# A decoder layer on one Trainium2 core: h and x1 transposed by VectorE in 32x32 squares instead of by TensorE

## The chip, the cores and the metric

The kernel runs on one core of one Trainium2 chip. The metric is the device time of one execution in microseconds (us), and the time of the kernel before is the median of three runs. The engines that matter are TensorE (PE; its weight loads are shown apart as PEld), VectorE (DVE), ScalarE (ACT), GpSimd (POOL) and SyncE (SP). SP, ACT and POOL each have a queue from which they issue DMA transfers ("SPq", "ACTq", "POOLq"); an engine takes its instructions, and its DMA issues with them, in the order in which they are written.

## The reference

One decoder layer for 16 sequences of 112 rows (1792 rows in all, 1024 wide), in three steps, each closed by a layer norm:

```
s  = silu(x @ Wg.T);  of each row the 1376 smallest |s| of 2752 stay, the others become 0
h  = s * (x @ Wu.T)                        # 1792 x 2752
x1 = norm(x + h @ Wd.T)                    # 1792 x 1024
x2 = norm(x1 + attention(x1 @ Wq, keys and values of a context of 375) @ Wo)
out = norm(x2 + x2 @ W4.T)                 # W4: 4-bit weights, unpacked, in bfloat16
```

All but the last product is in float32.

## The kernel before

The rows are 14 tiles of 128. Every engine runs its instructions in the order in which the code writes them (`as_written`, line 83). The stages that the change touches:

**Up stage** (`up_chunk` and `turn` in `gates_keys_up`, from line 100). For each tile and each of six chunks of 512, 512, 352, 512, 512 and 352 columns, TensorE computes x @ Wu (line 234) from xT, the tile's transposed rows, which SP loads (line 138, two buffers) when the next chunk is the first of a tile. SP also loads the gate's chunk `us` and the mask `um` (lines 211 and 212), POOL multiplies them (line 213), and VectorE multiplies the product in (line 241). `turn(n)` then makes h transposed, because the next product needs its columns on the partitions: four or three TensorE transposes of 128x128 into PSUM (line 255), ScalarE copies (lines 257 and 261) and stores on POOL's queue into the DRAM tile `hT_d` (lines 258 and 262). `emit` (line 395) fixes the order: the turn of chunk n-3 first, then the loads for chunk n+1 and the matmuls of chunk n, then the evacuation (the VectorE product) of chunk n-1. The gate's chunk has four buffers, so the load of `us` for chunk n+1 waits until chunk n-3 has been turned.

All this runs beside the search for each row's threshold (`count`, `update`, `finish`, lines 278 to 356): 31 counting steps a tile on ScalarE (line 284) and VectorE (lines 287 to 296), two tiles in turn, and then some ten pieces of longer work on VectorE and POOL. `beside` (line 424) spreads the stream of matmul chunks over the steps, by the width of each; an up chunk counts 1.07 of its width.

**Down** (class `Down`, from line 471). h @ Wd goes over pairs of tiles with seven products in place of eight. `block` (line 526) loads half a tile of transposed h by two DMAs on SP. `last_pass` (line 652) does, pair by pair: `load_rest` (line 646; SP loads two blocks for the pair after this one, VectorE adds them, lines 553 and 554), a first product of 22 matmuls, two additions on VectorE (lines 683 and 684), the first layer norm (`norm`, line 670, which also stores x1 by POOL's queue), `load_rows` (two loads of x on SP), a second product, a subtraction (line 689), the second norm, row sums on POOL for the next pair (`add_rows`, line 668), and then the steps of `beside[j]`: the unpacking of the 4-bit weights on VectorE (`compute`, lines 716 to 730), loads on ACT's queue, and the first transposes of x1.

**Queries** (from line 735). `fetch` loads 112 rows of x1 (`xr`, ACT's queue, one buffer), `rows` transposes them by eight TensorE transposes (line 757) and two ScalarE copies (line 758) into `x1T`, and `chunk` multiplies by Wq (line 765). Two sequences make a group; the loop of `attention_and_ffn` (from line 1053) spreads fetches, transposes and chunks of the next group over its units. Ahead of it SP loads the first keys and values and Wo (lines 811, 815 and 999); scores are line 832, and the squares that VectorE already makes of the probabilities line 860, stored by DMAs of 32 partitions (line 874).

The lines that set the order in the up stage:

```python
        while len(to_turn) > 1:
            turn(to_turn.popleft())
        evacuate = what()
        if evacuate:
            behind.append((evacuate, at if at >= 0 else None))
            settle(1)
```

Of the kernel before, what the change touches and what calls it, by code (L numbers as in the profile page):

```python
# [10 lines left out]
F32 = mybir.dt.float32  # L11
# [6 lines left out]
ALU = mybir.AluOpType  # L18
AX = mybir.AxisListType
PSUM = bass.MemoryType.PSUM  # L20
DRAM = bass.MemoryType.DRAM

P = 128
B, S, D = 16, 112, 1024
NT = B * S
TT = NT // P
KC = D // P
# [3 lines left out]
Q = 32  # L31
NKQ = -(-SK // Q)
SKP = NKQ * Q
NKP = -(-SK // P)
NH, NKV, HD = 32, 8, 32
REP = NH // NKV
KVD = NKV * HD
GB = 2
GT = GB * S
# [60 lines left out]
def gates_keys_up(  # L100
    nc, tc, ident, xT, wg, wu, ctxT, wk, wv, s_d, m_d, hT_d, k_d, v_d, down, left, ps_g, ps_t
):
# [142 lines left out]
    def turn(n):  # L245

        t, c = ups[n]
        off, w = UP_CHUNKS[c]
        h = sm.pop((t, c))
        k0, nk = off // FH * HK + off % FH // P, -(-w // P)  # L250
        pt = ps_t.tile([P, 4, P], F32, tag="pt", name=f"pt_{t}_{c}")
        hT = io.tile([P, 4, P], F32, tag="hT", name=f"hT_{t}_{c}", bufs=2)
        for k in range(nk):
            r = min(P, w - k * P)
            nc.tensor.transpose(pt[:r, k, :], h[:, ds(k * P, r)], ident)  # L255
        whole = w // P
        nc.scalar.copy(hT[:, :whole, :], pt[:, :whole, :])
        nc.gpsimd.dma_start(hT_d[t][:, k0 : k0 + whole, :], hT[:, :whole, :])
        if nk > whole:
            r = w % P  # L260
            nc.scalar.copy(hT[:r, whole, :], pt[:r, whole, :])
            nc.gpsimd.dma_start(hT_d[t][:r, k0 + whole, :], hT[:r, whole, :])

# [112 lines left out]
    for n, (t, c) in enumerate(ups):  # L376
        stream.append((UP_CHUNKS[c][1] * 1.07, lambda n=n: up_chunk(n)))
    found, pieces = set(), deque()
# [92 lines left out]
class Down:  # L471
# [14 lines left out]

    def __init__(self, nc, tc, negh, wd, hT_d, x, x1_d, ps):
        self.nc, self.tc, self.negh, self.wd, self.hT_d = nc, tc, negh, wd, hT_d
        self.x, self.x1_d, self.ps = x, x1_d, ps
        self.pairs = TT // 2  # L490
        self.parts = {"11": [], "21": []}
        self.asked = [(b, k) for b in ("11", "21") for k in range(HK)]
        self.n_blocks = 0
        self.live = {}
# [31 lines left out]
    def block(self, t, h):  # L526

        pool = (self.a1, self.a2)[self.n_blocks // 4 % 2] if self.a2 else self.a1
        self.n_blocks += 1
        a = pool.tile([P, HK, P], F32, tag="h", name=f"h_{self.n_blocks}", bufs=4)  # L530
        h_d = self.hT_d[t]
        self.nc.sync.dma_start(a[:, :FULL, :], h_d[:, ds(h * HK, FULL), :])
        self.nc.sync.dma_start(a[:REST, FULL, :], h_d[:REST, h * HK + FULL, :])
        return a
# [8 lines left out]
    def product(self, bank, a, b):  # L543
        for k in range(HK):
            r = P if k < FULL else REST
            self.nc.tensor.matmul(  # L546
                bank, a[:r, k, :], b(k)[:r],
                start=(k == 0), stop=(k == HK - 1),
            )
# [86 lines left out]
    def load_sums(self, j):  # L636

        v = self.nc.vector
        a11, a12, a21, a22 = (self.block(2 * j + i, h) for i in range(2) for h in range(2))
        self.combine(v, a22, a21, a22, ALU.add)  # L640
        self.combine(v, a21, a11, a21, ALU.subtract)
        self.combine(v, a22, a22, a11, ALU.subtract)
        self.combine(v, a12, a12, a22, ALU.subtract)
        self.live[j] = a22, a21, a12

    def load_rest(self, j):

        a21, a22 = (self.block(2 * j + 1, h) for h in range(2))
        self.combine(self.nc.vector, a21, a21, a22, ALU.add)
        self.live[j] = a21, a22  # L650

    def last_pass(self, beside):

        nc = self.nc
        with ExitStack() as ctx:
# [14 lines left out]
            def norm(j, i, y):  # L670
                layer_norm(nc, small, y, y, self.negh)
                nc.gpsimd.dma_start(self.x1_d[ts(2 * j + i, P), :], y)

            rows = {0: load_rows(0)}
            add_rows(0, rows[0])
            for j in range(self.pairs):
# [7 lines left out]
                nc.vector.tensor_add(y1[:, 512:], y1[:, 512:], p)  # L684
                norm(j, 0, y0)
                if j + 1 < self.pairs:
                    rows[j + 1] = load_rows(j + 1)
# [47 lines left out]
class Queries:  # L735


    def __init__(self, nc, tc, ctx, ident, x1_d, wq_sb, bank):
        self.nc, self.ident, self.x1_d, self.wq_sb, self.bank = nc, ident, x1_d, wq_sb, bank
        self.pool = ctx.enter_context(tc.tile_pool(name="q_work", bufs=1, side="right"))  # L740
        self.x1T, self.qT, self.xr = {}, {}, {}

    def fetch(self, g, bb):

        self.xr[g, bb] = self.pool.tile([S, D], F32, tag="xr", name=f"xr_{g}_{bb}")
        self.nc.scalar.dma_start(self.xr[g, bb], self.x1_d[ds((g * GB + bb) * S, S), :])

    def rows(self, g, bb):
        nc = self.nc
        if bb == 0:  # L750
            self.x1T[g] = self.pool.tile([P, KC, GT], F32, tag="x1T", name=f"x1T_{g}")
            self.qT[g] = self.pool.tile([P, KC, GT], F32, tag="qT", name=f"qT_{g}", bufs=2)
        xr = self.xr.pop((g, bb))
        for k0 in range(0, KC, 4):
            pt = self.bank()[:, : 4 * S].rearrange("p (k s) -> p k s", k=4)
            for k in range(4):
                nc.tensor.transpose(pt[:, k, :], xr[:, ts(k0 + k, P)], self.ident[:S, :S])  # L757
            nc.scalar.copy(self.x1T[g][:, k0 : k0 + 4, ts(bb, S)], pt)  # L758

    def chunk(self, g, mc):  # L760

        nc = self.nc
        pq = self.bank()
        for kc in range(KC):
            nc.tensor.matmul(  # L765
                pq[:, :GT], self.wq_sb[:, kc, ts(mc, P)], self.x1T[g][:, kc, :],
                start=(kc == 0), stop=(kc == KC - 1),
            )
        nc.scalar.activation(self.qT[g][:, mc, :], pq[:, :GT], AF.Copy, scale=SCALE)


def attention_and_ffn(nc, tc, ident, ident_b, negh, x1_d, k_d, v_d, queries, wf_sb, wo, out):
# [16 lines left out]
    with ExitStack() as ctx:  # L789
# [213 lines left out]
        asked, behind, light = deque((0, mc) for mc in range(EARLY, KC)), deque(), {}  # L1003
        turned, fetched = GB, GB
        sums, tails = {}, {}
# [47 lines left out]
        for n in range(n_units):  # L1053
# [16 lines left out]

            if not asked and turned < B and n >= (turned // GB - 1) * per_group:
                queries.rows(turned // GB, turned % GB)
                turned += 1
                if turned % GB == 0:
                    asked.extend((turned // GB - 1, mc) for mc in range(KC))
            if fetched == turned < B:
                queries.fetch(fetched // GB, fetched % GB)
                fetched += 1
            lights(n)
# [41 lines left out]
def kernel(  # L1121
# [30 lines left out]
    v_d = dram.tile([B, SKP, KVD], F32, tag="v", name="v_d")  # L1152
    x1_d = dram.tile([NT, D], F32, tag="x1", name="x1_d")

    hT_d = [dram.tile([P, 2 * HK, P], F32, tag=f"h{t}", name=f"hT_d{t}") for t in range(TT)]
    with as_written(nc, tc):
        with ExitStack() as psum:
            ps_g = psum.enter_context(tc.tile_pool(name="ps_g", bufs=6, space=PSUM))
            ps_t = psum.enter_context(tc.tile_pool(name="ps_t", bufs=2, space=PSUM))
            with ExitStack() as left:  # L1160
                down = Down(nc, tc, negh, wd, hT_d, x, x1_d, ps_g)
                gates_keys_up(
                    nc, tc, ident, xT, wg, wu, ctxT, wk, wv, s_d, m_d, hT_d, k_d, v_d, down, left,
                    ps_g, ps_t,
                )
# [3 lines left out]
                wf_sb = a_w.tile([P, 8, D], BF16, tag="wf", name="wf_sb")  # L1169
                queries = Queries(nc, tc, ctx, ident, x1_d, wq_sb, lambda: down.bank("pq"))  # L1170
                with tc.tile_pool(name="q", bufs=2, side="right") as q_pool:
# [4 lines left out]
                    loads, computes = unpack_steps(nc, q_pool, wf_sb, qw, qs, qz)  # L1176
                    beside = [[] for _ in range(TT // 2)]
                    for i, j in enumerate((1, 1, 2, 3, 4, 4, 5, 6)):
                        beside[j].append(computes[i])
                    for i, j in enumerate((0, 0, 1, 1, 2, 3, 4, 4)):  # L1180
                        beside[j].append(loads[i])
                    for i in range(4):
                        beside[i // 2].append(lambda i=i: load_wq(i))
                    beside[4].append(lambda: queries.fetch(0, 0))
                    beside[5] += [lambda: queries.rows(0, 0), lambda: queries.fetch(0, 1)]
                    beside[6].append(lambda: queries.rows(0, 1))
                    down.last_pass(beside)
            for mc in range(EARLY):
# [50 lines left out]
```

## Time and profile before

| | |
|---|---|
| median of three runs | 2656.92 us (2655.61 to 2657.28) |
| the profiled execution | 2661.48 us |
| its span, first to last instruction | 2659.7 us |
| PE busy | 2584.9 us (97%) |
| DVE busy | 1730.8 us (65%) |
| ACT busy | 1377.6 us (52%) |
| POOL busy | 1053.8 us (40%) |
| mean granted TensorE clock | 0.983 |
| up stage, by TensorE's order of time | 853.1 to 1404.7 us |
| last pass | 1735.3 to 1891.0 us |
| first scores of attention | 1901.95 us |

The profile is of one execution. Its page gives the busy time of each engine, the span in 40 slices, the DMA queues, the chain of work that ended last, and the costliest groups of instructions; the trace behind it can be asked for the order of time on each engine ("timeline": start, duration, and in brackets the idle time in front and what ended it), for the waits, and for the busy time and clock in any window. A group's line names the kernel's line, the engine, the operation and the tiles. TensorE's ends are modelled; its pitch, from start to start, is the safer number. A float32 matmul is two instructions.

### The profile page before, as it was taken

The page shows a single profiled execution, that of the slowest core. Times are in us where ns is not written, and L with a number is a line of the kernel's source. Part 1 is how long each engine was busy: PE and PEld are TensorE (multiplying, and loading weights), DVE is VectorE, ACT ScalarE, POOL GpSimd, SP SyncE. Part 2 cuts the span into 40 slices and gives each one's busy share as a digit, 9 for nine tenths or more (in the row PEclk, how much of TensorE's full clock was granted, in tenths as well). Part 3 has the DMA queues.
Part 4 walks back from the last instruction along what each step waited for, and adds up shares of the span by engine and source line. Part 5 has one row for each costly group of instructions (what it writes and reads, how often), then busy time and mean ns, then how long its engine had stood idle before and what let it go on. Part 6 is the DMA issues. An engine that isn't in the chain of part 4 may idle for free.

```text
span 2659.7 us, 33179 instructions
## 1 busy us (share of the span) xinstructions
PE 2584.9 (97%) x10266; PEld 1482.7 (56%) x10266; DVE 1730.8 (65%) x3579; ACT 1377.6 (52%) x2413; POOL 1053.8 (40%) x1097
## 2 busy tenths in 40 slices
PE   9999999999999999999999999998899999999997
PEld 4444444577776555555554444443556666667663
DVE  0478778866876788788730343158467777777773
ACT  0487787777767777787610000000255555565553
POOL 0002022213322444344450000023277888788783
PEclk9999999999999999999999999999889999999998
DMA  6221223154443543443346222166567777777763
GB/s 253 94 74 56 77 91 126 51 195 168 181 169 136 162 140 121 143 132 117 95 145 228 86 96 94 59 204 202 133 169 196 196 191 193 192 205 194 188 175 103
DMA packets 216960, 387.70 MB, mean 146 GB/s; under 512 B 32080, under 2 KB 151120, under 8 KB 212688
## 3 DMA queue, kind: packets, MB, share of 16 engines
q1 hardware_dynamic: 165456, 257.19, 32.3%
q0 software_dynamic: 35840, 100.59, 11.6%
q10 hardware_dynamic: 15488, 27.80, 3.5%
q8 instruction: 83, 1.36, 0.2%
q14 instruction: 93, 0.76, 0.1%
HBM read 208.36 MB, written 76.43 MB: 107 GB/s over the span
## 4 chain that ended last, share of the span: by engine, by line
PE 90%; DVE 3%; DMA 3%; ACT 2%; issue 1%; POOL 1%; ACTq 0%; SPq 0%; POOLq 0%; DVEq 0%
PE pg L146 20%; PE pu L234 19%; PE m L546 14%; PE bank L924 7%; PE pk L184 6%; PE pk L176 6%; PE bank L765 6%; PE sc L832 4%; PE po L887 3%; PE bank L975 2%; PE pt L255 1%; ACT probs L840 1%; DVE b L727 1%; DMA xr<-x_d 1%; DVE nmax L838 1%
## 5 line engine op out<-in xcount | busy, mean ns | idle before, releaser
L284 ACT ACTIVATE ja<-a,cand 128x1824 int8<-128x1824 f32 x434 | 788.6, 1817 | 178.4 <-DVE cand L296 174.4
L287 DVE TENSOR_SCALAR_CACHE_REDUCE jv<-a,cand 128x928 uint8<-128x928 f32 x434 | 510.0, 1175 | 56.9 <-ACT a L271 48.8
L234 PE MATMUL pu<-wu_sb,uxT 128*128 128x512 f32 (+1 forms) x1344 | 530.6, 548 | 0.0
L146 PE MATMUL pg<-wg_sb,gxT 128*128 128x456 f32 (+1 forms) x1344 | 519.9, 550 | 5.9 <-DMA wg_sb<-in_wg_dram 5.9
L840 ACT ACTIVATE probs<-sc,nmax 128x375 f32<-128x375 f32 x512 | 287.4, 573 | 237.6 <-DVE nmax L838 218.2
L146 PEld LDWEIGHTS pg<-wg_sb,gxT 128*128 128x128 f32 x1344 | 256.2, 191 | 268.8 <-issue 265.3
L849 POOL TENSOR_TENSOR probs<-probs,sums 128x1500 f32<-128x1500 f32 x128 | 344.2, 2689 | 142.4 <-DVE sums L848 123.2
L234 PEld LDWEIGHTS pu<-wu_sb,uxT 128*128 128x128 f32 x1344 | 249.0, 190 | 230.0 <-issue 188.4
L838 DVE TENSOR_REDUCE nmax<-sc 128x2 f32<-128x750 f32 x256 | 228.6, 932 | 150.3 <-PE sc L832 150.2
L546 PE MATMUL m<-wd,h 128*128 128x512 f32 (+1 forms) x616 | 268.0, 597 | 0.0
L860 DVE STREAM_TRANSPOSE squares<-probs 128x1536 f32<-128x1536 f32 x128 | 224.0, 1750 | 9.7 <-DMA weights<-squares 5.5
L155 POOL DMA_DIRECT2D s_d<-s x84 | 46.0, 548 | 427.4 <-DVE s L154 351.5
L765 PE MATMUL bank<-x1T,wq_sb 128*128 128x224 f32 x976 | 202.6, 361 | 0.0
L546 PEld LDWEIGHTS m<-wd,h 128*128 128x128 f32 (+1 forms) x616 | 117.5, 191 | 149.2 <-issue 145.1
L765 PEld LDWEIGHTS bank<-x1T,wq_sb 128*128 128x128 f32 x976 | 181.3, 191 | 33.2 <-issue 30.2
L924 PE MATMUL bank<-wo_sb,aT 128*128 128x256 f32 x832 | 195.0, 388 | 0.0
L758 ACT COPY x1T<-pq 128x448 f32<-128x448 f32 x4 | 2.0, 535 | 371.6 <-PE pq L757 371.6
L874 POOL DMA_DIRECT2D weights<-squares x320 | 178.6, 564 | 9.0 <-issue 6.6
L924 PEld LDWEIGHTS bank<-wo_sb,aT 128*128 128x128 f32 x832 | 155.4, 192 | 46.5 <-issue 24.9
L184 PE MATMUL pk<-wv_sb,ctx 128*128 128x256 f32 (+1 forms) x768 | 168.4, 379 | 0.0
L176 PE MATMUL pk<-ctx,wk_sb 128*128 128x375 f32 x512 | 164.4, 478 | 0.0
L184 PEld LDWEIGHTS pk<-wv_sb,ctx 128*128 128x128 f32 (+1 forms) x768 | 144.0, 188 | 24.8
(118 smaller groups left out, 2881.8 us busy)
## 6 DMA issues: line engine op xcount, KB each, us to landing
weights<-squares SPq DMA_DIRECT2D x704, 96.0 KB, 3.3
h<-hT_d SPq DMA_DIRECT2D x56, 640.0 KB, 4.5
weights<-squares POOLq DMA_DIRECT2D x320, 96.0 KB, 3.4
ctx<-in_ctxT_dram SPq DMA_DIRECT2D x16, 1500.0 KB, 6.7
a<-s_d SPq DMA_DIRECT2D x14, 1376.0 KB, 7.9
us<-s_d SPq DMA_DIRECT2D x56, 256.0 KB, 2.7
hT_d<-hT POOLq DMA_DIRECT2D x56, 256.0 KB, 3.1
s_d<-s POOLq DMA_DIRECT2D x56, 228.0 KB, 2.2
```

Source lines behind the costliest of these rows:

```text
L146: nc.tensor.matmul(pg[:, :w], xts[t][:, kc, :], wg_sb[:, kc, ds(off, w)], start=(kc == 0), stop=(kc == KC - 1),)
L176: nc.tensor.matmul(pk[:, :SK], wk_sb[:, kc, ts(u, P)], c[:, kc, :], start=(kc == 0), stop=(kc == KC - 1),)
L184: nc.tensor.matmul(pk[:n, :KVD], c[:, kc, ds(at, n)], wv_sb[:, kc, :], start=(kc == 0), stop=(kc == KC - 1),)
L234: nc.tensor.matmul(pu[:, :w], xts[t][:, kc, :], wu_sb[0][:, kc, ds(off, w)], start=(kc == 0), stop=(kc == KC - 1),)
L284: nc.scalar.activation(ja, a[:, NV:], AF.Sign, bias=cand, scale=-1.0, accum_out=st["sgn"])
L287: nc.vector.tensor_scalar(jv, a[:, :NV], cand, -(TOPK - 1 - NA / 2), ALU.is_lt, ALU.add, accum_out=st["nlt"])
L546: self.nc.tensor.matmul(bank, a[:r, k, :], b(k)[:r], start=(k == 0), stop=(k == HK - 1),)
L765: nc.tensor.matmul(pq[:, :GT], self.wq_sb[:, kc, ts(mc, P)], self.x1T[g][:, kc, :], start=(kc == 0), stop=(kc == KC - 1),)
L838: nc.vector.tensor_reduce(nmax[h], sc[h][:, :, :SK], AX.X, ALU.max, negate=True)
L840: nc.scalar.activation(pr[:, i, :SK], sc[i // 2][:, i % 2, :SK], AF.Exp, bias=nmax[i // 2][:, i % 2 : i % 2 + 1], accum_out=sums[:, i : i ...
L849: nc.gpsimd.tensor_tensor(pr, pr, sums.unsqueeze(2).to_broadcast([P, 4, SK]), ALU.mult)
L924: nc.tensor.matmul(pp[:, :256], aT[:, h, r, :], wo_sb[:, h * REP + r, ts(i, 256)], start=(h == 0 and r == 0), stop=(h == 1 and r == REP - 1),)
```

## The change

- `turn` no longer uses TensorE. VectorE transposes each 32x32 square of the chunk (one instruction, two for the 352-wide chunks), writing with a step of 4 or 3 elements so that the squares of a row lie together; POOL sets the padding of the last chunk to zero; four DMAs of 32 partitions, two on SP's queue and two on POOL's, put the squares into place in `hT_d`. The two PSUM buffers of the transposes go to the matmuls (6 to 8), and an up chunk counts its plain width in the stream.
- A block of h is loaded by one DMA, its columns are read by the down products with a step of 4 or 3 elements, and sums over blocks are one instruction instead of two.
- `norm` in the last pass transposes x1 too: two VectorE instructions a tile, into dead accumulators, and eight DMAs on SP's queue into a new DRAM tile `x1T_d`. The transposes, copies and fetches of Queries go; `load` takes a whole group by one DMA on ACT's queue, and the loop asks for it when the chunks of the group before are all written.
- The unpacking stands between the two products of a pair (`amid`, after the first norm), no longer behind the second norm.

```diff
@@ turn
-        pt = ps_t.tile([P, 4, P], F32, tag="pt", name=f"pt_{t}_{c}")
-        hT = io.tile([P, 4, P], F32, tag="hT", name=f"hT_{t}_{c}", bufs=2)
-        for k in range(nk):
-            r = min(P, w - k * P)
-            nc.tensor.transpose(pt[:r, k, :], h[:, ds(k * P, r)], ident)
-        whole = w // P
-        nc.scalar.copy(hT[:, :whole, :], pt[:, :whole, :])
-        nc.gpsimd.dma_start(hT_d[t][:, k0 : k0 + whole, :], hT[:, :whole, :])
...
+        at, whole, nk = off % FH, w // P, -(-w // P)
+        tile = io.tile([P, 512], F32, tag="hT", name=f"hsq_{t}_{c}", bufs=2)
+        sq = tile[:, : nk * P].rearrange("p (m f k) -> p m k f", m=SQ, k=nk)
+        nc.vector.transpose(
+            sq[:, :, :whole],
+            h[:, : whole * P].rearrange("p (k m f) -> p m k f", m=SQ, f=Q),
+        )
         if nk > whole:
...
+            n = w % P // Q
+            nc.gpsimd.memset(sq[:, n:, whole], 0.0)
+            nc.vector.transpose(
+                sq[:, :n, whole], h[:, whole * P : w].rearrange("p (m f) -> p m f", f=Q)
+            )
+        n = nk * Q
+        to = hT_d[t].rearrange("(m p) h n -> p m h n", p=Q)
+        for b in range(SQ):
+            queue = (nc.sync, nc.gpsimd)[b % 2]
+            queue.dma_start(
+                to[:, :, off // FH, ds(at + b * n, n)],
+                tile[ts(b, Q), : nk * P].rearrange("p (m n) -> p m n", m=SQ),
+            )
@@ the stream
-        stream.append((UP_CHUNKS[c][1] * 1.07, lambda n=n: up_chunk(n)))
+        stream.append((UP_CHUNKS[c][1], lambda n=n: up_chunk(n)))
@@ Down.block, Down.product
-        self.nc.sync.dma_start(a[:, :FULL, :], h_d[:, ds(h * HK, FULL), :])
-        self.nc.sync.dma_start(a[:REST, FULL, :], h_d[:REST, h * HK + FULL, :])
+        self.nc.sync.dma_start(a, self.hT_d[t][:, h])
...
+            at, n = k // 4 * 4 * P, min(4, HK - k // 4 * 4)
             self.nc.tensor.matmul(
-                bank, a[:r, k, :], b(k)[:r],
+                bank, a[:r, ds(at + k - at // P, P, n)], b(k)[:r],
@@ Down.last_pass
             def norm(j, i, y):
                 layer_norm(nc, small, y, y, self.negh)
-                nc.gpsimd.dma_start(self.x1_d[ts(2 * j + i, P), :], y)
+                t = 2 * j + i
+                nc.gpsimd.dma_start(self.x1_d[ts(t, P), :], y)
+                to = self.x1T_d.rearrange("(m p) b k f -> p m b k f", p=Q)
+                n = KC // 2
+                for h in range(2):
+                    sq = ((self.c11[j], self.v[j]), (self.u[j], None))[i][h]
+                    if sq is None:
+                        sq = ld.tile([P, 512], F32, tag="sq", name=f"x1sq_{t}", bufs=1)
+                    sq = sq.rearrange("p (m k f) -> p m k f", m=SQ, f=Q)
+                    nc.vector.transpose(
+                        sq, y[:, ts(h, 512)].rearrange("p (k m f) -> p m k f", m=SQ, f=Q)
+                    )
+                    for b in range(SQ):
+                        nc.sync.dma_start(to[:, :, t * SQ + b, ts(h, n)], sq[ts(b, Q)])
...
                 norm(j, 0, y0)
+                for step in amid[j]:
+                    step()
                 if j + 1 < self.pairs:
                     rows[j + 1] = load_rows(j + 1)
@@ Queries (fetch and rows go)
+    def load(self, g):
+        n = GT // Q
+        self.x1T[g] = self.pool.tile([P, n, KC, Q], F32, tag="x1T", name=f"x1T_{g}")
+        self.nc.scalar.dma_start(self.x1T[g], self.x1T_d[:, ts(g, n)])
...
-                pq[:, :GT], self.wq_sb[:, kc, ts(mc, P)], self.x1T[g][:, kc, :],
+                pq[:, :GT].rearrange("p (b f) -> p b f", f=Q), self.wq_sb[:, kc, ts(mc, P)],
+                self.x1T[g][:, :, kc, :],
@@ the loop of attention_and_ffn
-            if not asked and turned < B and n >= (turned // GB - 1) * per_group:
-                queries.rows(turned // GB, turned % GB)
-                turned += 1
-                if turned % GB == 0:
-                    asked.extend((turned // GB - 1, mc) for mc in range(KC))
-            if fetched == turned < B:
-                queries.fetch(fetched // GB, fetched % GB)
-                fetched += 1
+            if not asked and group < B // GB:
+                if group not in queries.x1T:
+                    queries.load(group)
+                elif n >= (group - 1) * per_group:
+                    asked.extend((group, mc) for mc in range(KC))
+                    group += 1
@@ tile_decoder_kernel
-            ps_g = psum.enter_context(tc.tile_pool(name="ps_g", bufs=6, space=PSUM))
-            ps_t = psum.enter_context(tc.tile_pool(name="ps_t", bufs=2, space=PSUM))
+            ps_g = psum.enter_context(tc.tile_pool(name="ps_g", bufs=8, space=PSUM))
...
                     for i, j in enumerate((1, 1, 2, 3, 4, 4, 5, 6)):
-                        beside[j].append(computes[i])
+                        amid[j].append(computes[i])
...
-                    beside[4].append(lambda: queries.fetch(0, 0))
-                    beside[5] += [lambda: queries.rows(0, 0), lambda: queries.fetch(0, 1)]
-                    beside[6].append(lambda: queries.rows(0, 1))
+                    beside[4].append(lambda: queries.load(0))
```

## The prediction

> **What bounds the kernel now.** I read the chain of work that ended last first, then TensorE's order of time in each stage, then the queue that feeds it (SyncE), then VectorE. The page's chain:
>
> ```profile
> PE 90%; DVE 3%; DMA 3%; ACT 2%; issue 1%; POOL 1%; ACTq 0%; SPq 0%; POOLq 0%; DVEq 0%
> ```
>
> TensorE carries the end nearly everywhere, so an instruction taken from it is worth its pitch, and a new wait of TensorE costs its full length. Its order of time at one tile boundary of the up stage (start, duration; 3-4 transposes stand between the chunks):
>
> ```profile
> 1115.44 7.03 PE L234 MATMUL pu<-wu_sb,uxT 128*128 128x512 f32 x16
> ...
> 1122.64 4.90 PE L234 MATMUL pu<-wu_sb,uxT 128*128 128x352 f32 x16
> 1127.38 0.60 PE L255 MATMUL pt<-ident,us 128*128 128x128 f32 x4
> 1127.81 7.03 PE L234 MATMUL pu<-wu_sb,uxT 128*128 128x512 f32 x16
> ```
>
> SyncE and VectorE at the same place: the next tile's xT is issued when TensorE starts chunk 4 of the old tile (1115.4), 11.3 us before its use at 1127.81; VectorE does chunk 4's product only at 1130.39, 7.9 us after TensorE ended it (1122.5).
>
> ```profile
> 1116.48 0.42 SPq L138 DMA_DIRECT2D uxT<-in_xT_dram  x1
> ```
> ```profile
> 1130.39 0.66 DVE L241 TENSOR_TENSOR us<-us,pu 128x512 f32<-128x512 f32 x1
> ```
>
> VectorE lags because the search's last pieces (3.1, 1.6, 1.6, four of 1.6 us ...) come in a bunch. Today that lag costs nothing, since SyncE waits for TensorE's transposes, hardly for VectorE (its queue's waits between 870 and 1330: total, times, longest):
>
> ```profile
> SPq L211 <- PE pt L255: 358.0, 69, 6.4
> SPq L212 <- DMA m_d<-m: 12.5, 1, 12.5
> SPq L211 <- DVE us L241: 10.8, 9, 2.9
> ```
>
> The last pass, and its one long stall:
>
> ```profile
> 1735.33 114.19 PE L546 MATMUL m<-wd,h 128*128 128x512 f32 x264
> 1868.20 1.73 PE L757 MATMUL pq<-ident,xr 112*128 112x112 f32 x8 [18.68 <-DMA xr<-x_d]
> 1869.72 21.43 PE L546 MATMUL m<-wd,h 128*128 128x512 f32 x44
> ```
>
> Six pairs take 114.2 us dense (a pair of 44 matmuls 18.9, by the chain's 359.15 us for 836); then the x1 transposes that stand in front of the last pair wait 18.7 us, and the clock, at 0.50 to 0.55 from 1865 to 1875 by the windows, makes the last pair 2.5 us longer.
>
> **The change part by part.** Durations are of the profiled execution (2661.5 us; span 2659.7); it is 4.6 above the median of 2656.9, and I put the differences on the median.
>
> *Up stage, removed.* From 853.1 to 1404.7 is 551.6 us; the matmuls alone are 28 x (6.87+6.87+4.74) = 517.4. The transposes are the rest: -34 us. ScalarE's 112 copies (L257, L261) go too; ScalarE is no bound, worth nothing.
>
> *Up stage, added: VectorE's squares.* The only row of such an instruction:
>
> ```profile
> L860 DVE STREAM_TRANSPOSE squares<-probs x128: 1741/1748/1779, 1916.1 to 2607.0; 128x1536 f32<-128x1536 f32 x128
> ```
>
> 1.75 us for 1536 elements, about 0.14 of it fixed: 0.67 for 512, at a pitch of 0.60 (as L241, of the same size: 0.69, pitch 0.60), some 3.4 us a tile. Its squares leave in runs of 32; the new ones leave with a step of 3 or 4 elements, which no VectorE row shows. Ends: 0.60, and 1.22 by the slowest VectorE row per element (the scan L334, 1.64 for 688); faster than L860's rate is excluded, since nothing here is narrower. I take 0.60: L860 is the same operation. Beside POOL's work L860 never grows (1779 at most).
>
> *Up stage, moved: SyncE.* Two of four stores of each chunk now stand on SyncE, waiting for VectorE, and the load of the next tile's xT is queued behind those of chunk 2. The instruction order shows VectorE turning chunk 2 directly in front of its product of chunk 4. So xT can be issued only when VectorE gets to chunk 4's product, plus two issues of 0.60 (L874, the nearest DMA of 32 partitions; low end 0.32 of L211), plus 4.9 to land: reach + 6.1 us. I held that against the start of the next tile on TensorE in the trace of before. At five boundaries VectorE is early (idle 1 to 2 us in front of the product): no stall. At the others the product starts at 888.67, 970.35, 1050.46, 1130.39, 1164.74, 1202.36, 1242.56 and 1323.47, and the next tile at 891.71, 970.41, 1049.11, 1127.81, 1167.16, 1206.51, 1245.86 and 1324.56: with 6.1 added TensorE would wait 3.1, 6.0, 7.5, 8.7, 3.7, 2.0, 2.8 and 5.0, in all 39 us. In the three long lags VectorE also has about 0.6 more and TensorE 0.4 less a chunk, over four chunks: 3 x 4 = 12. Together about +50 (25 if xT lands in the fastest 3.8 and the issues are 0.32, so that each wait is 1.7 shorter and VectorE's squares find room; 75 with squares of 1.2 and the 2.5 us of slow clock behind each long stall). **Net of the stage: +16.** The lighter weight of an up chunk (1.07 to 1.0) gives 3% more search to the gate stage, where VectorE is 71 to 82% busy: nothing. The padding (28 memsets) and 56 more POOL issues at 0.55 us fall on a POOL 40 to 52% busy: nothing, unless the squares wait for them.
>
> *The strided weights.* The down products read h with a step of 12 or 16 bytes. Nearest rows: L968 loads strided weights (step 16 bytes, bf16) in 150 ns, L975 contiguous ones in 103. In that ratio 190 becomes 277 ns, under the 427 ns pitch of a 512 matmul: nothing; a gain is excluded, since the load is already hidden. Uncovered from 427 ns on. Queries' moving operand in runs of 32: L887 does so at 391 ns against 388 of L924: nothing. The Trainium skill, "SBUF — State Buffer", section "Door 1: The DMA port swizzle", says that SBUF is read in lines of 16 bytes and that each access to a new line pays; it speaks against both strides. It gives no price; by it the squares would sit at their dear end and the sum at 2708 below, by L860's row it stays at 2671.
>
> *Last pass.* PE loses the stall. But SyncE gets 16 stores a pair, and the loads of the pair after next (load_rest) stand behind the last eight, which wait for VectorE's squares of the pair's second norm; VectorE's next instruction is the sum of just these loads. That closes a loop, per pair: sum 1.6, adds and first norm 4.4 (1745.05 to 1749.45), squares 1.3, unpack 4.3 each (1895.04 to 1899.4, without POOL's rows beside it), second norm 3.9, first square 0.7, eight stores 4.8, load 0.4+4.5+0.4: 22 us + 4.3 per unpack, against TensorE's 18.9. Counted from the pass's start (1735.3): third pair's sum ready at 35, then 66 (two unpacks), 92, 118, 149 (two): last pair starts at 149, not 113. POOL's row sums for it (behind the norms of the pair before) end at about 167; from there 4.4 + 1.3 + 4.3 + 3.9 + 0.7 bring its last norm's squares to 182, eight stores to 187, and only then does SyncE load the first keys: first scores at 190. Before: 1901.95 - 1735.3 = 167. **+23** (issue 0.33: +11; if SyncE never blocks: first scores at 132 + 9.4 + 0.5 = 142, **-25**). Unpacking away from POOL's row sums (5.7 us for an L727 that takes 0.69 alone) is worth 5 us an unpack on VectorE and is in the loop.
>
> *Attention.* 14 groups of eight transposes, 0.87 apart from what follows, go (-12), and waits for xr of 10.7 us, with some 2 us of slow clock behind the longest (matmul groups of 1.76 and 1.63 for 0.93 and 0.91): **-25**. x1T is fetched as one load when the last chunk has read the old one, one to three units ahead; a unit is 4 to 6 us, a load of 896 KB some 6 to 9 (512 KB: 5.1): I take nothing, end +8.
>
> **Sum:** +16 +23 -25 = +14: 2657 + 14 = **2671 us**.
>
> **Rivals.**
> - *Neither queue wait shows* (SyncE's stores are quick, VectorE's lag shrinks with ScalarE's freed copies): -34 -25 -25 = -84: 2573. For it: VectorE is idle 16 to 20% of the up stage. Against: the lag at the boundaries stands in the trace. 0.08.
> - *One of the two shows*: xT alone (+16 -25 -25): 2623, or the last pass alone (-34 +23 -25): 2621. It ends faster, and decides it where one loop is short: xT landing within 3.8 and issued at 0.32 each leaves only three boundaries late. 0.20.
> - *VectorE becomes the bound*: at squares of 1.2 us the up stage has 84 x 0.6 = 50 us more VectorE work, of which some 20 fall in lags, and the last pass 28 x 0.6 = 17 in its loop: 2671 + 20 + 17 = 2708. It decides from squares of about 1 us. 0.14.
> - *The forecast*, both waits, 2634 to 2704 by its bounds (-34 +25 +11 -25 and -34 +75 +23 -17): 0.58.
>
> **How the numbers follow.** 0.2% (5.3 us) is about what a measurement of this kernel can tell from no change: 2651.6 to 2662.2. Of the forecast's 0.58, 0.41 lies above, 0.11 inside, 0.06 below. Slower 0.41+0.14 = 0.55; same 0.11; faster 0.06+0.20+0.08 = 0.34. Range 2615 to 2715: it leaves out the first rival and a little above.
>
> **What would show it.** TensorE idle in front of chunk 0 of tiles 2, 4 and 6 on uxT, 5 to 10 us each, with half clock after: if it is idle nowhere between 853 and 1390 the second step is wrong. TensorE idle 7 to 12 us in front of pairs 3 to 6 on VectorE's sum of h, and SyncE idle on the squares; kT as the first scores' releaser. L256 at 0.67 us for 512, or more. L757 gone and no wait on x1T in attention. Wrong I should be if a DMA is not held by those in front of it on SyncE, or the landing times differ by a few us.

## The result, and the profile after

The changed kernel takes 2775.62 us (median of 4 runs, 2774.39 to 2777.74), the kernel before 2657.1 us beside it (2655.61 to 2659.72): ratio 1.0446, 95% interval [1.0428, 1.0464]. The forecast of 2671 us had the sign right and the size far too small; the range ended at 2715. In the profiled executions the spans are 2772.6 and 2659.7 us, 112.9 apart, and the stages divide them so (from TensorE's order of time; the up stage is counted to the first down product):

| us | up stage | first passes | last pass to first scores | attention | span |
|---|---|---|---|---|---|
| before | 551.6 | 330.6 | 166.6 | 757.8 | 2659.7 |
| after | 622.2 | 330.8 | 208.5 | 758.0 | 2772.6 |
| difference | +70.6 | +0.2 | +41.9 | +0.2 | +112.9 |
| forecast | +16 | 0 | +23 | -25 | +14 |

The chain of work that ended last, on the page after:

```profile
PE 66%; DVE 11%; DMA 8%; issue 4%; POOL 4%; ACT 3%; SPq 3%; ACTq 0%; DVEq 0%; POOLq 0%
```

It was 90% TensorE; a third of the time (34%, a tenth before) now runs through other engines' work, much of it in front of a waiting TensorE. Before, TensorE had no wait in front of a matmul of the up stage; now it waits at nine tile starts, 84.5 us in all (total, times, longest):

```profile
PE pu L235 <- DMA uxT<-in_xT_dram: 59.9, 5, 19.2
PE pu L235 <- DVE hsq L256: 20.3, 3, 8.7
PE pu L235 <- DVE rej L306: 4.4, 1, 4.4
```

What SyncE's queue waited for between 870 and 1330 us (total, times, longest), where it used to wait for TensorE's transposes:

```profile
SPq L270 <- DVE hsq L263: 131.7, 21, 13.4
SPq L270 <- DVE hsq L256: 89.1, 23, 9.0
SPq L270 <- DVE us L242: 78.4, 16, 13.1
SPq L270 <- POOL hsq L262: 29.0, 6, 10.0
```

The first three are the forecast's step: stores waiting for VectorE. The fourth is not in it. L262 is the padding of the last chunk's squares, set to zero by POOL. One of the three longest waits of TensorE, from four orders of time around 1060 us (VectorE's squares of a chunk 2 from after's line 263; POOL; SyncE; TensorE):

```profile
1059.07 0.26 DVE L263 STREAM_TRANSPOSE hsq<-us 128x96 f32<-128x96 f32 x1
```
```profile
1065.25 1.48 POOL L358 TENSOR_TENSOR e<-e,c 128x688 bf16<-128x688 bf16 x1
1066.81 1.49 POOL L359 TENSOR_TENSOR m<-m,e 128x688 bf16<-128x688 bf16 x1
1068.59 0.60 POOL L361 DMA_DIRECT2D m_d<-m  x1 [0.30 <-POOL m L359]
1069.19 0.16 POOL L262 MEMSET hsq<- 128x32 f32 x1
```
```profile
1069.37 1.99 SPq L270 DMA_DIRECT2D hT_d<-hsq  x2
1071.45 0.39 SPq L139 DMA_DIRECT2D uxT<-in_xT_dram  x1
```
```profile
1076.35 6.17 PE L235 MATMUL pu<-wu_sb,uxT 128*128 128x512 f32 x8 [18.62 <-DMA uxT<-in_xT_dram]
```

The squares were done at 1059.3. Their store could not go before the padding was set, the padding stood on POOL behind the search's masks (eight of 1.49 us), and xT stood on SyncE behind the store: the store goes out 10.0 us late, and xT with it, for an instruction that takes 0.16. It happens again at 1378 and 1431, 7.3 and 16.1 us late, in front of waits of 19.25 and 13.18 us. Meanwhile TensorE's granted clock falls to 0.53 (1060 to 1076 us).

VectorE's squares of h and of x1 (the second row is one of the four groups of L694):

```profile
L256 DVE STREAM_TRANSPOSE hsq<-us x84: 503/1091/1161, 876.6 to 1480.3; 128x512 f32<-128x512 f32 x56, 128x256 f32<-128x256 f32 x28
```
```profile
L694 DVE STREAM_TRANSPOSE v<-y 128x512 f32<-128x512 f32 x7 | 4.7, 669 | 0.0
```

Same operation, same 512 elements: 1.09 us written with a step of 4, 0.67 in runs of 32 (0.71 in two of the four groups). The last pass on TensorE:

```profile
1847.72 21.67 PE L557 MATMUL m<-wd,h 128*128 128x512 f32 x44 [3.82 <-DVE h L660]
1882.47 21.37 PE L557 MATMUL m<-wd,h 128*128 128x512 f32 x44 [13.07 <-DVE h L660]
1910.33 21.09 PE L557 MATMUL m<-wd,h 128*128 128x512 f32 x44 [6.49 <-DVE h L660]
1939.42 21.90 PE L557 MATMUL m<-wd,h 128*128 128x512 f32 x44 [8.00 <-DVE h L660]
1974.97 21.20 PE L557 MATMUL m<-wd,h 128*128 128x512 f32 x44 [13.66 <-DVE h L660]
...
2014.56 1.63 PE L852 MATMUL sc<-kT,qT 32*128 32x375 f32 x8 [9.31 <-DMA kT<-k_d]
```

Five waits (45 us) for the sum of h and one for the first keys, as foretold, but each round is some us longer.

### The profile page after: what moved, and what is told of

It reads as the page before. It is cut to its first block, busy times and chain, and to the rows that moved or that the text cites. A ratio compares the mean times of both kernels' runs of the same rounds, so it can differ in the third digit from the quotient of the medians.

```text
span 2772.6 us, 32454 instructions
## 1 busy us (share of the span) xinstructions
PE 2562.8 (92%) x9816; PEld 1554.1 (56%) x9830; DVE 1785.4 (64%) x3684; ACT 1318.7 (48%) x2269; POOL 1076.2 (39%) x1181
## 4 chain that ended last, share of the span: by engine, by line
PE 66%; DVE 11%; DMA 8%; issue 4%; POOL 4%; ACT 3%; SPq 3%; ACTq 0%; DVEq 0%; POOLq 0%
PE pg L147 18%; PE m L557 12%; PE pu L235 8%; PE pk L177 5%; PE pk L185 5%; PE bank L944 5%; PE bank L784 4%; PE sc L852 3%; PE po L907 3%; DVE jv L298 3%; PE bank L995 2%; SPq L894 1%; ACT probs L860 1%; DMA h<-hT_d 1%; DMA weights<-squares 1%
## 5 line engine op out<-in xcount | busy, mean ns | idle before, releaser
L235 PE MATMUL pu<-wu_sb,uxT 128*128 128x512 f32 (+1 forms) x1344 | 537.9, 563 | 84.5 <-DMA uxT<-in_xT_dram 59.9
L235 PEld LDWEIGHTS pu<-wu_sb,uxT 128*128 128x128 f32 x1344 | 261.6, 195 | 360.5 <-issue 280.1
L860 ACT ACTIVATE probs<-sc,nmax 128x375 f32<-128x375 f32 x512 | 286.3, 571 | 250.1 <-DVE nmax L858 234.0
L557 PE MATMUL m<-wd,h 128*128 128x512 f32 (+1 forms) x616 | 277.6, 613 | 45.0 <-DVE h L660 45.0
L557 PEld LDWEIGHTS m<-wd,h 128*128 128x128 f32 (+1 forms) x616 | 180.6, 294 | 141.5 <-DVE h L660 48.9
L880 DVE STREAM_TRANSPOSE squares<-probs 128x1536 f32<-128x1536 f32 x128 | 224.2, 1751 | 28.1 <-DMA weights<-squares 16.1
L214 POOL TENSOR_TENSOR us<-us,um 128x512 f32<-128x512 f32 (+1 forms) x84 | 91.0, 1084 | 197.0 <-DMA um<-m_d 196.7
L852 PE MATMUL sc<-kT,qT 32*128 32x375 f32 x1024 | 140.7, 545 | 26.8 <-DMA kT<-k_d 17.3
```

The lines of the kernel that those rows point to most:

```text
L235: nc.tensor.matmul(pu[:, :w], xts[t][:, kc, :], wu_sb[0][:, kc, ds(off, w)], start=(kc == 0), stop=(kc == KC - 1),)
L557: self.nc.tensor.matmul(bank, a[:r, ds(at + k - at // P, P, n)], b(k)[:r], start=(k == 0), stop=(k == HK - 1),)
L860: nc.scalar.activation(pr[:, i, :SK], sc[i // 2][:, i % 2, :SK], AF.Exp, bias=nmax[i // 2][:, i % 2 : i % 2 + 1], accum_out=sums[:, i : i ...
L880: nc.vector.transpose(sq[:, :, n % 2].rearrange("p k (i f) -> p k i f", f=Q), probs[:, n % 3].rearrange("p i (k f) -> p k i f", f=Q),)
```

## The experiments

All against the kernel after unless said otherwise. "Idle" is what TensorE waits for the first block of h at the end of the up stage; it is part of the stage.

| run | up stage (idle) | last pass | attention | median us | ratio to before [95%] |
|---|---|---|---|---|---|
| e1_plain | 615.8 | 206.8 | 757.2 | 2766.92 | 1.0411 [1.0394, 1.0429] |
| e2_early | 553.2 (16.6) | 205.4 | 757.8 | 2707.93 | 1.0197 [1.0180, 1.0214] |
| e3_act | 624.4 | 202.6 | 762.4 | 2769.68 | 1.0427 [1.0410, 1.0443] |
| e4_x1only | 551.6 | 210.7 | 746.3 | 2693.97 | 1.0141 [1.0124, 1.0157] |
| e5_ask | 622.9 | 180.8 | 762.2 | 2748.29 | 1.0334 [1.0314, 1.0354] |
| e6_up | 549.7 (14.8) | 206.3 | 753.9 | 2697.67 | 1.0145 [1.0121, 1.0170] |
| e7_best | 548.2 (16.1) | 179.3 | 760.6 | 2676.77 | 1.0074 [1.0046, 1.0101] |
| e8_noload | 624.3 | 206.5 | 737.9 | 2754.54 | 1.0358 [1.0341, 1.0375] |
| e9_up_plain | 541.2 (15.2) | 206.2 | 758.0 | 2692.32 | 1.0131 [1.0104, 1.0158] |
| e10_beside | 547.8 (15.9) | 177.1 | 750.9 | 2674.58 | 1.0072 [1.0046, 1.0098] |
| e12_best2 | 535.2 | 172.4 | 776.3 | 2665.24 | 1.0028 [1.0014, 1.0042] |
| e13_pad | 576.2 | 203.2 | 757.4 | 2726.35 | 1.0265 [1.0249, 1.0281] |
| e14_best3 | 525.5 | 181.1 | 753.5 | 2651.66 | 0.9975 [0.9962, 0.9988] |

**e1_plain: squares of h without the step.**

```diff
-sq = tile[:, : nk * P].rearrange("p (m f k) -> p m k f", m=SQ, k=nk)
+sq = tile[:, : nk * P].rearrange("p (m k f) -> p m k f", m=SQ, k=nk)
```

> The squares of h are written without the step of 4 (32 elements in a row), everything else as after; so the columns of h come to the down products in the wrong order, and the output is not the reference's. Theory A (the step is what costs): L256 falls from 1.09 us to about 0.67 to 0.71 for 512, as L694 takes for its 512, VectorE gets some 35 us back over the up stage (84 x 0.42), and the stage falls from 622 us to about 585, the whole from 2776 to about 2740. Theory B (the order on SyncE's queue costs: xT of the next tile stands behind the stores of the squares): TensorE still waits some 60 us for uxT, the stage falls by less than 15 us and the whole stays over 2760.

L256 fell to a mean of 0.62 us (from 0.91), but the stage only by 6.4 us, and TensorE still waited 77.5 us in it (84.5 after). Theory A falls: VectorE's dear squares lie beside other work, worth 8.7 us in all.

**e2_early: xT asked three chunks earlier.**

```diff
-        if c == 0:
-            load_x(t, "u")
+        if n == 0:
+            load_x(0, "u")
+        if c == 3 and t + 1 < TT:
+            load_x(t + 1, "u")
```

> xT of the next tile of the up stage is asked three chunks earlier (with the loads of chunk 3 instead of those of the next tile's chunk 0), everything else as after. Theory B (the order on SyncE's queue): TensorE's waits for uxT, 59.9 us, go almost wholly and nothing takes their place, the up stage falls from 622 to about 565 us and the whole to about 2717. Theory A (VectorE's strided squares set the pace): the waits move to the squares and the products behind them (47 us before), the stage stays over 600 us and the whole over 2750.

67.7 us less, where theory B had 59. TensorE's waits in the up stage fall from 84.5 to 14.1 us, and those put down to "hsq L256" went with those for uxT: they stood at tile starts and had been waits for xT as well. (The 47 us in the expectation are 20.3 of TensorE's matmuls and 26.6 of its weight loads, which wait at the same places, so they are not to be added to the 59.9.)

```profile
PE m L559 <- DMA h<-hT_d: 16.8, 1, 16.8
PE pu L237 <- DMA uxT<-in_xT_dram: 14.1, 4, 6.4
```

The products now end at 536.6, but the first block of h comes 16.6 us later, so the stage as a whole is at 553.

**e3_act: x1's stores on ScalarE's queue.**

```diff
-nc.sync.dma_start(to[:, :, t * SQ + b, ts(h, n)], sq[ts(b, Q)])
+nc.scalar.dma_start(to[:, :, t * SQ + b, ts(h, n)], sq[ts(b, Q)])
```

> The sixteen stores of x1's squares per pair are issued by ScalarE instead of SyncE, everything else as after. Theory C (the loop over SyncE: load_rest stands behind the stores, VectorE's next sum behind load_rest): TensorE's waits for the sum of h in the last pass, 45 us, fall to under 10, the time from the pass's start to the first scores falls from 209 to about 165 us or less, and the 9 us wait for the first keys goes too: about 2732. Theory D (VectorE's own work in the last pass, squares and unpacking and norms, is what is late): the stretch falls by less than 12 us and the whole stays over 2763. In attention the waits for v and for the weights (13 us) fall if they are left over from SyncE's stores, and stay if not.

Only 5.9 us less. h came early, yet the pairs waited 42 us, now behind two other things:

```profile
1890.01 0.23 DVE L747 CAST zf<-zi 128x128 f32<-128x128 int32 x1 [11.12 <-DMA zi<-in_qz_dram]
...
1899.46 6.05 DVE L660 TENSOR_TENSOR h<-h,h 128x1408 f32<-128x1408 f32 x1
```

The unpacking's loads stand on ScalarE's queue and were now behind the stores; and the sum of h, 1.6 us alone, takes 6.05 beside POOL's row sums. So the total is the one that theory D named, but what was late was in part the loads behind the moved stores: neither C nor D was tested cleanly.

**e5_ask: the loads of h issued ahead of the second stores, which stay on SyncE.**

```diff
                 nc.vector.tensor_tensor(y1[:, :512], y1[:, :512], q, ALU.subtract)
+                if j + 2 < self.pairs:
+                    self.ask_rest(j + 2)
                 norm(j, 1, y1)
```

> In the last pass the two loads of h for the pair after next are issued on SyncE ahead of the stores of the second x1 tile's squares instead of behind them; the stores stay on SyncE, everything else as after. Theory C (the loop over SyncE's order): TensorE's 45 us of waits for the sum of h fall to under 12, pass start to first scores from 209 to about 175, whole about 2742. Theory D (VectorE's own work per pair, 22 to 26 us with its sum of 4 to 6 us where POOL adds rows at the same time, against TensorE's 18.9): waits stay over 25 us, the stretch over 190, the whole over 2757.

The stretch fell by 27.7 us to 180.8 and the waits for h from 45.0 to 20.6. The loop over SyncE is most of the loss (theory C, which expected 175); some 5 us a pair in four pairs stay, and the 9.3 us wait for the keys, which still stand behind the last stores.

**e4_x1only: h as before, x1 and the queries as after.** The edit puts `turn`, `block`, `product` and the sums of h back.

> h is transposed as before (TensorE, ScalarE's copies, two DMAs a block), only x1, the queries and the place of the unpacking are as after. If the parts simply add (up stage +71, last pass +42, attention 0 by the two traces): up stage back at 552 us, last pass to first scores 209, about 2699. If the last pass is late because of the up stage or of h's form (the strided weights, the one-instruction sums): first scores nearer to 167 us after the pass's start, and 2657 to 2675. If attention's missing gain (25 us expected) was lost to h's part: about 2674.

Up stage 551.6, last pass 210.7: the parts add. x1's part costs 37 us alone, h's the other 82. Attention is 11.7 us shorter here than after, though its code is the same; e8 bears on that.

**e6_up, e7_best: early xT and four buffers for h's squares; the same with e5's edit.**

```diff
-        tile = io.tile([P, 512], F32, tag="hT", name=f"hsq_{t}_{c}", bufs=2)
+        tile = io.tile([P, 512], F32, tag="hT", name=f"hsq_{t}_{c}", bufs=4)
```

> xT asked three chunks earlier, as in the run with the early xT (2708), and four buffers for h's squares instead of two. If the two buffers, held by stores that POOL issues behind its own work, were the rest of the up stage's loss: VectorE's waits for its own stores (60 us) fall to under 10, the 17 us wait for h at the end of the stage goes, the stage from 553 to about 535 us, the whole to about 2690. If the two buffers cost nothing (VectorE's wait is hidden, and what is late at the end is SyncE's queue): stage over 550, whole 2704 to 2710.

> The three mends together: xT earlier, four buffers for h's squares, the loads of h ahead of the stores in the last pass. If they add as their theories have it: 2776 - 69 - 18 - 34, about 2655, the same as before. If VectorE's own work bounds the last pass: about 2680.

VectorE's waits for its own stores went, and the stage gained 3.5 us (the whole 10, some of it in attention): the time moved to waits of VectorE for POOL's products. The idle 15 us at the end stayed. Together: 2677, where e6 less the 27 us of e5 would be 2670; the mends nearly add, without the 18 us expected of the buffers. That this lies near the 2680 of the other theory is chance: the last pass took 179.3 us, as short as in e5.

**e8_noload: attention without the loads of groups 1 to 7.**

```diff
+        if g:
+            self.x1T[g] = self.x1T[0]
+            return
```

> The loads of x1's transposed groups 1 to 7 are left out: the queries of all groups are made from group 0, so the output is not the reference's. Everything else as after. If those loads (one DMA of 0.9 MB each) are what takes attention's gain back, by colliding with the loads of v and the stores of the weights: attention from the first scores to the end falls from 758 to about 738 us and TensorE's waits for v and the weights (13 us) go. If not: attention stays at 754 us or more with the same waits, and the gain was lost to TensorE's pace with ScalarE, VectorE and POOL.

Attention fell by 20.1 us, as the colliding loads would have it. In the kernel after, a load is issued at 2198.41 and TensorE waits for the values:

```profile
2198.41 0.33 ACTq L775 DMA_DIRECT2D x1T<-x1T_d  x1
```
```profile
2205.15 2.78 PE L907 MATMUL po<-weights,v 128*32 128x256 f32 x24 [5.66 <-DMA v<-v_d]
```

Within 20 us of the other loads stand waits for kT (7.94, 8 us after the load at 2036.8), v (1.50) and the weights (1.09, 1.31, 3.63); inside attention the three kinds come to 21 us. (Before the change they came to 7.8, 6.8 of them for the same second keys.) Without the loads they come to 1.7 us:

```profile
PE sc L855 <- DMA kT<-k_d: 10.1, 2, 9.3
...
PE po L910 <- DMA weights<-squares: 0.9, 1, 0.9
```

(9.3 of the first line lie in front of the first scores.)

**e9_up_plain: e6 with the squares of e1.**

> xT earlier and four buffers, as in the run of that pair (2698), and the squares of h written without the step of 4, so that h's columns are in the wrong order and the output is not the reference's. If VectorE's strided squares are what is left (they delay the search of the last rows, and with it the mask that the last chunks need): the last mask and the first load of h come 20 to 35 us earlier, the 15 us wait for h goes and the whole falls to about 2675. If VectorE has slack in the up stage (ScalarE's counts or the steps of the search set the pace): the wait for h stays over 10 us and the whole within 6 us of 2698.

2692.32 against 2697.67, with overlapping intervals, and the idle 15.2 us stay: VectorE's squares do not bound the stage even when xT no longer does.

**e10_beside: e7 with the unpacking back behind the second norm.**

```diff
-                        amid[j].append(computes[i])
+                        beside[j].append(computes[i])
```

> The three mends as in the run of them together (2677), and the unpacking put back behind the second norm and POOL's row sums, where it stood before the change. If unpacking beside POOL's row sums costs VectorE 5 us an unpack, as forecast: the last pass grows from 179 to 190 us or more, whole 2688 or more. If its place is without effect: whole within 5 us of 2677.

2674.58 against 2676.77, last pass 177.1 against 179.3: the place has no effect here. But the price of 5 us was mostly not met, so the run does not refute it. In the kernel before, VectorE's subtraction in an unpack runs beside POOL's row sums:

```profile
1801.30 5.70 DVE L727 TENSOR_TENSOR b<-b,zf 128x512 f32<-128x512 int32 x1
```
```profile
1801.50 1.28 POOL L668 TENSOR_TENSOR y<-y,c 128x512 f32<-128x512 f32 x1
```

In e10 the row sums wait 3.9 to 9.7 us for the rows of x, and in the three rounds with one unpack they begin when it is over (the last instruction of an unpack; the first row sum after it):

```profile
1810.61 0.69 DVE L766 TENSOR_TENSOR wf_sb<-b,sc 128x512 bf16<-128x512 f32 x1
```
```profile
1816.37 1.25 POOL L687 TENSOR_TENSOR y<-y,c 128x512 f32<-128x512 f32 x1 [9.73 <-DMA y<-in_x_dram]
```

In the two rounds with two unpacks they do meet, and there the unpacking takes some 4 us longer (8.6 us for the second unpack from 1785.96, against 4.3 for the first).

**e12_best2: e7, the first blocks of h asked ahead of the last chunks, and the last pair's stores on GpSimd.**

```diff
     to_load.extend(down.settle(left))
+    down.first_blocks()
...
+                        queue = nc.gpsimd if j + 1 == self.pairs else nc.sync
```

> The three mends (2677) and two more: the first three blocks of h are asked ahead of the last chunks of the up stage instead of behind them, and the last pair's stores of x1's squares are issued by GpSimd. If the 15 us wait for h is only the order on SyncE, and the first keys' wait of 8 us only the stores ahead of them: 2677 - 15 - 8, about 2654, no different from before. If h comes late because the last chunks themselves do: 2664 to 2670.

The idle time at the end of the up stage is gone (it was only SyncE's order), and the first scores come 7 us earlier in the pass. The 2665 lies in the range of the other expectation, but not for its reason: in attention a new wait of 13.3 us for the probabilities stands 20 us after the first scores, and attention grew to 776 us; that GpSimd's normalisation stood behind its new stores is argued, not shown.

**e13_pad: the padding set by VectorE.**

```diff
-            nc.gpsimd.memset(sq[:, n:, whole], 0.0)
+            nc.vector.memset(sq[:, n:, whole], 0.0)
```

> The padding of h's last squares is set by VectorE instead of GpSimd, everything else as after. Theory E (the long waits for xT, 18.6, 19.3 and 13.2 us, come from the padding: it stands on GpSimd behind the masks of the search, 12 us, SyncE's store waits for it and xT stands behind that store): those three fall by 33 us together to at most 10 each, the up stage from 622 to about 590 us, the whole from 2776 to about 2743, and the short waits of 4 to 9 us at the other tiles stay. Theory F (VectorE is held by its two buffers, whose stores stand on GpSimd behind the masks too): the long waits stay, the whole stays over 2765.

49 us less, 46 of them in the up stage. TensorE's waits in the stage fall from 84.5 to 43.1 us:

```profile
PE pu L235 <- DMA uxT<-in_xT_dram: 16.9, 4, 7.0
PE pu L235 <- DVE us L242: 11.8, 2, 8.5
PE pu L235 <- DVE jv L298: 10.0, 1, 10.0
PE pu L235 <- DVE next L301: 4.4, 1, 4.4
```

The three long ones fall from 51.1 us together to 17.1 (7.05, 10.01 and none), close to the 33 us of theory E; the other six fall from 33.5 to 26.0. The last 4.6 of the 46 are in the matmuls themselves, which are busy 533.3 us instead of 537.9; around a long wait the granted clock is low (after: 0.50 in the wait from 1376 to 1384.5 us, 0.63 in the 5.5 us behind it). The tile whose orders of time were shown after the change now goes so (SyncE; TensorE):

```profile
1053.70 0.80 SPq L270 DMA_DIRECT2D hT_d<-hsq  x2
1054.62 0.35 SPq L139 DMA_DIRECT2D uxT<-in_xT_dram  x1
```
```profile
1058.60 21.91 PE L235 MATMUL pu<-wu_sb,uxT 128*128 128x512 f32 x50 [7.05 <-DMA uxT<-in_xT_dram]
```

VectorE's squares of that chunk end at 1053.67 and the store goes at once, while POOL's masks are still running (1048.5 to 1062.6). A wait of 7.05 stays, where the forecast had 7.5 for this tile. Theory F falls.

**e14_best3: early xT, padding by VectorE, e5's order, the first blocks earlier; two buffers, all x1 stores on SyncE.**

> xT three chunks earlier, the padding by VectorE, the loads of h ahead of the stores in the last pass, and the first three blocks of h asked ahead of the last chunks; two buffers for h's squares as after. If the stages add as measured one by one (up stage 532 to 536 without a gap behind it, passes 331, last pass 179, attention 758): 853 + 534 + 331 + 179 + 758 = 2655, no different from before. If the two buffers matter once xT no longer does: the up stage over 545, 2666 or more. Faster than before (under 2650) only if attention, too, comes out at 750 or less.

2651.66 us, 0.25% under before, at the edge of what can be told, and near the 2655 that the stages add up to. The up stage is 525.5, 26 us better than before, with two buffers. In e12, which also has xT and the first blocks early but the padding on POOL (and four buffers), it is 535.2: so with xT early the padding is worth some 10 us, against 46 with xT behind it; no run changes it alone there.

## Why the prediction was wrong

The forecast's difference of spans was +14, the measured one +112.9. The 99 us between them by its steps:

- **The padding, costed at "nothing, unless the squares wait for them": 46 us, the step that failed.** They wait, or rather their stores do. The step looked at POOL's busy share (40 to 52%) and not at what stands in front of the padding on POOL's queue, nor at what waits behind it: store, xT, TensorE. Changing only the padding's engine takes 46.0 us out of the stage (e13), 41.4 of them waits of TensorE.
- **xT behind the stores: mechanism right, size nearly.** With the padding out of the way the stage is 24.6 us over before, where the forecast had +16 net, and TensorE waits 43.1 us at eight tile starts, seven of them among the forecast's eight, which added up to 39. (Its sign named tiles 2, 4 and 6; the starts it had worked out, 970.41, 1049.11 and 1127.81, are those of tiles 3, 5 and 7 counted from 0, which waited 5.0, 18.6 and 8.7 us after the change.) That the order on SyncE is nearly the whole of it is shown by e2: with xT asked early, TensorE's waits in the stage fall from 84.5 us to 14.1.
- **The removal, -34: 26 of it is there.** It shows only when nothing waits (e14: 525.5; the forecast's floor was 517.4).
- **Squares at 0.60 pitch: wrong, and it hardly mattered.** They take 1.09 us (0.70 without the step, e1). The rival that priced VectorE as the bound set its point at 1 us and its price at 37; the squares passed the point, and the price was 8.7 us (e1). Of the 37, the 17 for the last pass could not fall due: x1's squares are written in runs of 32 and take 0.67 to 0.71. The row L860 that the forecast trusted writes runs of 32. The Trainium skill, "SBUF — State Buffer", section "Door 1: The DMA port swizzle", says that each access that crosses to a new 16-byte line pays, and the trace agrees here: the write with a step of 16 bytes is 1.5 to 1.6 times the contiguous one.
- **Strided weights: right.** L557 loads them in 294 ns on average, 298 for the full 128x128 (191 before; 277 estimated), hidden under matmuls of 427; the first passes take 330.8 us against 330.6.
- **Last pass, +23: right loop, 19 us too short.** Some 6.6 us lie in front of the third pair, whose sum of h is ready 41.6 us into the pass, where 35 had been added up; there eight stores took 8.4 us (from 1831.17), not 4.8. The four rounds behind it add 13.5: with one unpack they took 27.9 us (sum of h from 1880.79 to 1908.64) and 29.1 where 26.3 had been added up, with two 34.8 and 35.6 for 30.6. From there to the first scores it went 1.4 us faster than added up. In the first with one, eight stores took 5.5 us, not 4.8, and h landed 5.9 us after its first issue, not 5.3. e5 shows the loop: take load_rest out of it and 27.7 us go. That the place of the unpacking is worth 5 us an unpack was not borne out: put back, it cost nothing (e10), since POOL's row sums mostly missed it. Where the two meet the price is there (5.70 us for 0.69 before the change).
- **Attention, -25: lost.** The transposes and their waits are gone, and TensorE is 15 us less busy (by its records, of which 14 are missing after), but it waits for v, the weights and kT instead (21 us, 7.8 before). The load of x1T was taken at nothing, with an end of +8; e8 puts it at 20 us. Whether xr's loads caused the waits before was not tested, and loading x1T early into a second buffer was not tried. Why attention, with the same code, took 746 to 762 us in the profiles of kernels that differ only ahead of it stays open; its waits for v and the weights differ from one to the next.

46 + 9 + 19 + 25 make the 99.

The rivals: neither queue wait and one queue wait fall, since both loops are there (e2, e5); VectorE as the bound falls (e1, e9). The second rival's condition does not follow from the forecast's own figures either: 1.7 us off each of its eight waits leaves all eight late, not only three.

## What to carry to other kernels

Before an instruction is costed at nothing, ask what stands in front of it on its queue and who waits behind it: 0.16 us at a time on a half-idle engine cost 46 us, because a store, a load on another queue and TensorE hung on it in turn. A load that the critical engine needs should not stand behind a store that waits for another engine; issue it first, and the order alone was worth 68 us here and 28 in the last pass. Moving x1's stores to another queue moved the wait here to what that queue already carried (e3).

## What the runs showed of the hardware

- VectorE's 32x32 transposes of 512 float32 elements: 0.67 to 0.71 us written in runs of 32, 1.09 with a step of 4. TensorE's weight loads of 128x128 float32: 191 ns contiguous, 298 with a step of 3 or 4.
- VectorE's sum of 1408 elements takes 1.6 us alone and took 6.05 while POOL added rows (e3: four adds, 5 us).
- Four DMA issues of x1's stores on SyncE took 1.77 to 5.41 us in the last pass (four from 1897.18: 3.54; the next four: 1.83).
